# Half of the sums x1 + lam y of half 0 made beside y of half 1, from the x1 that is loaded there

## The chip, the cores and the metric

The kernel runs on one core of one Trainium2 chip. The metric is device time in microseconds, from one launch to its end; a kernel's time is the median of its runs. Beside the timed runs there is one profiled execution, taken by the hardware profiler, and all rows quoted here come from it. The engines are TensorE (PE, with its weight loads as PEld), VectorE (DVE), ScalarE (ACT), GpSimd (POOL) and SyncE (SP). SP and POOL issue most DMAs (rows named SPq are SP's issues).

## The reference, cut to what matters

The input is one image of 256 x 256 pixels and 128 channels in float32. Layer 0 is a row-wise attention with a residual; its result is `x1`. Layer 1 takes the group-normed `x1` as 256 tokens (its first axis), each an image of 256 x 128 points, runs a spectral attention over them and then two spectral mixing layers:

```python
attn = fno_layer(attn, p_wr, p_wi, p_bias, p_sw, p_sb, (H, W))
attn = instance_norm(attn + tokens, attn_norm_w, attn_norm_b)
attn = attn.reshape(b * (C // TOKEN_CODIM), TOKEN_CODIM, H, W)
h0 = instance_norm(attn, norm2_w, norm2_b)
h1 = fno_layer(h0, mix_wr[0], mix_wi[0], mix_bias[0], mix_sw[0], mix_sb[0], (H, W), norm=True, act=True)
h2 = fno_layer(h1, mix_wr[1], mix_wi[1], mix_bias[1], mix_sw[1], mix_sb[1], (H, W), norm=True)
out = instance_norm(h2, mon_w, mon_b) + attn
...
x = x + _L1_conv_ref(_gn(x), ...)
```

In the kernel's names `y` is `attn + tokens` before its instance norm (the group norm is folded into the matrices), and that norm is `lam y` plus a constant. The last two lines therefore need, at every pixel, the sum `w = x1 + lam y`; `lam` is one number per token, known only when all of a token's `y` has been made and its variance taken. `norm(h2)` is added to `w` at the very end.

## The kernel before

The 256 tokens are treated as two halves of 128 (`a` = 0 and 1), one token per partition. A half has 16 blocks of `NB` = 2048 pixels, or 32 half blocks `u` of `HB` = 1024. The order of each engine's instructions from `y_blocks` on is the order in which the Python code emits them (`manual_schedule`); the tile framework adds the semaphore waits, also those that come from memory which is used again: a pool that opens after another one has closed takes over its memory, and its first writes wait for the last use of what lay there.

The stages that matter here run in this order (L1813 on):

* `y_blocks(0, ...)`: y of half 0, 32 half blocks, kept whole in the SBUF tile `blocks` (16 x 2048 per partition; `hb[b]` is block b).
* `mp0`, the pool of the first modes: `y_blocks(1, br, 0, 24)` makes y of half 1 for u = 0 to 23, woven with `first_modes(0, ...)`. After that y goes on alone (`run(y1)`).
* `hp0`, the pool of the first images: `first_images(0, ...)`, 16 blocks.
* `mp1`: y of half 1 for u = 24 to 31 with `second_modes(0)` and `first_modes(1)`, then the images and outputs of both halves.

**y_blocks** (L1327). For a half block u, SP loads x1 of all 256 tokens (`load_x1`, tag "xt", three buffers, two loads of 512 KB each) and, every second u, the modes `gs`. The load for u + 2 is emitted at the top of u, so it reuses the buffer of u - 1. TensorE makes 16 products with `mpT` (L1351) and 16 small ones from the modes (L1219) into four PSUM banks; DVE scales them into y (L1361, `yt`) and takes statistics (L1363). For half 1, POOL then stores y to DRAM (L1365, `yd`, 512 KB).

**first_modes** (L1441) takes the variance of y of half 0, makes `lam` (column 3 of `h.col`) in a chain of small DVE steps with two square roots on ACT, scales F, and runs `mix_modes` (L1368): 16 products `x0m` (L1387), each summed into PSUM by TensorE (`x0acc`, L1400). Of the 16, those with number 2, 5, 8, 11 and 14 are on POOL, the others on DVE. `mixed` (L1405) copies the two sums into one tile `x0Z` of tag "f" (ACT L1410, DVE L1411), and `synth_modes` turns it into modes in four chunks (TensorE `g10gp` L609, copies `g10gt` of tag "gt" L617, stores to `Gd1` by POOL and ACT L622). `weave` (L1250) draws the next half block of y whenever the steps of the modes have used up the 4.2 us that a half block is counted with.

**first_images** (L1510) for half 0. Per block b: SP loads the modes `gs2` (L1243, four loads of 64 KB) and the two halves of x1 (`load_w`, L1530, 512 KB each, tiles of tags "yt" and "xw"); TensorE makes `ups` from block b (L1234 and L1219); ACT applies gelu in place into `blocks` (L1560); TensorE transposes the block before (`htps`, L1572), DVE copies it (L1584, L1575), TensorE makes `sps` (DVE statistics, L1592) and `psA` (L1595), ACT copies that into `yA` (L1597), POOL stores it (L1598, `Yd`). Beside this, `add_w` makes the sums w one block ahead, before gelu overwrites y: ACT scales y by lam (L1537), POOL adds the x1 (L1540) and stores the sum to the DRAM tile `wd` (L1541, 512 KB). Much later `output_0` loads `wd` again (L1733).

Of the kernel before, what the change touches and what calls it, by code (L numbers as in the profile page):

```python
# [18 lines left out]
P = 128  # L19
# [526 lines left out]
def layer1(tc, I, C, ident, x1d, upool, U, stats2, groups, out):  # L546
# [9 lines left out]
    with ExitStack() as ctx:  # L556
# [705 lines left out]
        def run(stage):  # L1262
            for _ in stage:
                pass
# [51 lines left out]
        for a in range(2):  # L1316
            h = Half()
            halves.append(h)
            h.col = sp.tile([P, 16], FP, name=f"col_{a}")
            h.turn = sp.tile([P, 8], FP, name=f"turn_{a}")  # L1320
            h.bl0 = sp.tile([P, P], FP, name=f"bl0_{a}")
            h.Gd1 = dram.tile([32, 4, 64, P], FP, name=f"Gd1_{a}")
            h.Gd2 = dram.tile([32, 4, 64, P], FP, name=f"Gd2_{a}")
            h.Yd = dram.tile([H, 32, P], FP, name=f"Yd_{a}")
        wd = dram.tile([P, 16 * NB], FP, name="wd")

        def y_blocks(a, psum, lo, hi, kept=16):  # L1327

            tt = slice(a * P, (a + 1) * P)
            gs = {}  # L1330

            def load(u):
                if (a, u) not in xts:
                    xts[a, u] = load_x1(a, u)
                if u % 2 == 0:
                    gs[u // 2] = xp.tile([P, 4, P], FP, tag="gs", name=f"gs_{a}_{u}", bufs=3)
                    load_modes(gs[u // 2], Gd0, u // 2, tt)

            load(lo)
            load(lo + 1)  # L1340
            yield 0.0
            for u in range(lo, hi):
                b, s = u // 2, u % 2
                if u + 2 < hi:
                    load(u + 2)
                xt = xts.pop((a, u))
                ps = [psum.pool.tile([P, 512], FP, tag=psum.tag, name=f"yps_{a}_{u}_{j}") for j in range(4)]
                ps = [z[:, 0:256] for z in ps]
                for j in range(4):
                    for sc in range(2):  # L1350
                        nc.tensor.matmul(  # L1351
                            rows_of(ps[j]), mpT[:, sc, tt], by_turn(xt[:, sc])[:, j],
                            start=(sc == 0), stop=False,
                        )
                image(ps, gs[b], bsy, range(2 * s, 2 * s + 2))
                if a == 0:
                    yt = blocks[:, b, s * HB : (s + 1) * HB]
                else:
                    yt = xp.tile([P, HB], FP, tag="yt", name=f"yt_{u}")
                for j in range(4):  # L1360
                    nc.vector.tensor_tensor(by_turn(yt)[:, j], rows_of(ps[j]), bc(rwb, 1, 2), ALU.mult)  # L1361
                for g in range(2):
                    nc.vector.bn_stats(ystat[:, a, 2 * u + g, :], yt[:, g * 512 : (g + 1) * 512])  # L1363
                if a:
                    nc.gpsimd.dma_start(ydv[:, a, u * HB : (u + 1) * HB], yt)  # L1365
                yield 4.2

        def mix_modes(mk, acc, F, l, tag, cs):  # L1368

# [71 lines left out]
        def first_modes(a, wp, mk, psum, gts):  # L1441

            h = halves[a]
            F = mk("F", [P, 4, 2, P], f"F0_{a}")
            nc.sync.dma_start(
                F.rearrange("p c r t -> p (c r) t"),
                Fyd[:, :, :, a * P : (a + 1) * P].rearrange("p c r t -> p (c r) t"),
            )
            dg = mk("m", [P, 2, P], f"dg3_{a}")
            ym, yv, ra, lam, r2, rho, sig = (h.col[:, k : k + 1] for k in range(7))  # L1450
            nc.vector.bn_aggr(h.col[:, 0:2], ystat[:, a].rearrange("p k s -> p (k s)"))
            yield 1.0
            rsqrt(nc, wp, ra, yv, EPS, "rq")
            nc.vector.tensor_mul(lam, ra, an[:, 0:1])
            nc.vector.tensor_mul(r2, lam, lam)
            nc.vector.tensor_mul(r2, r2, yv)
            yield 1.8
            rsqrt(nc, wp, r2, r2, EPS, "rq")
            nc.vector.tensor_mul(rho, lam, r2)
            nc.vector.tensor_mul(rho, rho, ch[:, 0:1])  # L1460
            nc.vector.tensor_mul(sig, ym, rho)
            nc.vector.tensor_sub(sig, ch[:, 1:2], sig)
            nc.vector.tensor_scalar(dg[:, 0, :], ident, rho, None, ALU.mult)
            nc.vector.tensor_scalar(dg[:, 1, :], ident, sig, None, ALU.mult)
            nc.vector.tensor_scalar(h.bl0, blk[0], rho, None, ALU.mult)
            yield 2.7
            ps = psum.tile(f"rhops_{a}")
            nc.tensor.matmul(ps[:, 0:256], ones, dg.rearrange("p k t -> p (k t)"), start=True, stop=True)
            yield 0.9
            rb = mk("m", [P, 256], f"rb_{a}")  # L1470
            nc.vector.tensor_copy(rb, ps[:, 0:256])
            f8 = F.rearrange("p c r t -> p (c r) t")
            nc.vector.tensor_tensor(f8, f8, bc(rb[:, 0:P], 1, 8), ALU.mult)
            nc.vector.tensor_add(F[0:1, 0, 0, :], F[0:1, 0, 0, :], rb[0:1, P:])
            yield 1.8
            acc = [psum.tile(f"x{a}acc_{r}") for r in range(2)]
            yield from mix_modes(mk, acc, F, 0, f"x{a}", range(4))
            Z, sq = mixed(mk, acc, f"x{a}")
            yield 1.2
            tail = norm(wp, mk, psum, h, sq, f"x{a}")  # L1480
            for c in range(4):
                synth_modes(wp, psum.pool, Z, P, h.Gd1, f"g1{a}", turned=True, chunk=c, ptag=psum.tag, gts=gts,
                            queues=(nc.gpsimd, nc.scalar))
                yield 2.4
                if c == 0:
                    yield next(tail)
                    yield next(tail)
                if c == 1:
                    run(tail)
                    nc.vector.tensor_mul(h.bl0, h.bl0, h.row[:, 0:P])  # L1490

                    ps = h.row
                    nc.tensor.matmul(ps[:, 256:257], blk[0], sig, start=True, stop=False)
                    nc.tensor.matmul(ps[:, 256:257], ident, ch[:, 2:3], start=False, stop=True)
                    nc.vector.tensor_copy(h.col[:, 13:14], ps[:, 256:257])
                    turned = mk("m", [P, 4, P], f"turned_{a}")
                    for j in range(4):
                        t = turned[:, j].rearrange("k (b d x) -> k b d x", b=2, d=2)
                        nc.vector.tensor_copy(
                            t[:, :: (-1 if j & 2 else 1), :: (-1 if j & 1 else 1)],  # L1500
                            ident.rearrange("k (b d x) -> k b d x", b=2, d=2),
                        )
                    for j in range(4):
                        nc.tensor.matmul(
                            ps[:, 260 + 2 * j : 262 + 2 * j], turned[:, j], h.col[:, 12:14],
                            start=True, stop=True,
                        )
                    nc.vector.tensor_copy(h.turn, ps[:, 260:268])

        def first_images(a, wp, yp, psk, pst, first=None):  # L1510
# [14 lines left out]

            def load_w(b):
                for s in range(2):
                    t = (yp, "yt", 2) if s == 0 else (wp, "xw", 1)
                    ys[b, s] = t[0].tile([P, HB], FP, tag=t[1], name=f"xw_{b}_{s}", bufs=t[2])
                    nc.sync.dma_start(ys[b, s], x1v[:, a, b * NB + s * HB : b * NB + (s + 1) * HB])  # L1530

            def add_w(b):

                t = yp.tile([P, NB], FP, tag="xt", name=f"w0_{b}", bufs=3)
                for s in range(2):
                    px = slice(s * HB, (s + 1) * HB)
                    nc.scalar.activation(t[:, px], hb[b][:, px], AF.Identity, scale=h.col[:, 3:4])  # L1537
                for s in range(2):
                    px = slice(s * HB, (s + 1) * HB)
                    nc.gpsimd.tensor_tensor(t[:, px], t[:, px], ys.pop((b, s)), ALU.add)  # L1540
                    nc.gpsimd.dma_start(wd[:, b * NB + s * HB : b * NB + (s + 1) * HB], t[:, px])  # L1541
# [271 lines left out]
        with tc.manual_schedule(engines=COMPUTE | {ENG.SP}):  # L1813
# [8 lines left out]
            with yctx:  # L1822
                U1 = 24
                with tc.tile_pool(name="mp0", bufs=1) as wp:
                    y1 = y_blocks(1, br, 0, U1)
                    weave((2.4 * t for t in first_modes(0, wp, tiles(wp), bq, [(wp, "gt", 1)])), y1)
                    run(y1)
                with tc.tile_pool(name="hp0", bufs=2) as wp:
                    run(first_images(0, wp, xp, bq, br))
# [226 lines left out]
```

## Time and profile before

| what | value |
|---|---|
| time, median of 3 runs | 2884.54 us (2880.02 to 2887.79) |
| the profiled execution's own time | 2878.79 us |
| its span | 2877.0 us |
| busy: PE, DVE, ACT, POOL | 2643.1, 2004.2, 1488.4, 1679.6 us |
| first and last y of half 1 in `mp0` (start of the DVE row) | 2036.4 and 2190.2 us |
| last row of half 0's images (psA) | 2327.0 to 2328.0 us |
| DMA of the span | 430.12 MB, 149 GB/s on average |

The span is the time between the first and the last instruction of the profiled execution; the device time lies 1.8 us above it. A row of the timeline has its start, its duration, the engine, the line, the operation with output and inputs, and in brackets how long the engine had been idle and what ended that. In a group's row, "busy" and "mean ns" are followed by the idle time before the group's instructions and its releasers. In the table by stretch there is one row per stretch of the span.

### The profile page before, as it was taken

Reading aid. Unit: us, or ns where it says so; the run is one execution under the profiler, and the core shown is the slowest. Engines: PE = TensorE matmul, PEld = TensorE weight load, DVE = VectorE, ACT = ScalarE, POOL = GpSimd, SP = SyncE. Lnnn points to the kernel's source line nnn. Section 1 sums busy time; section 2 is a strip of 40 time slices with the busy share of each in tenths; the row PEclk is TensorE's granted clock in tenths of the full one; section 3 lists DMA queues with packets and bytes.
Section 4 is the critical chain, followed back from the end, with each engine's and each line's share of the span. In section 5 each row is a group of like instructions: output and inputs, shape, how many; then the busy total and the mean of one; then the engine's idle time right before and its main releaser. Section 6 shows DMA issues by size and latency. Waiting matters only on the chain. (4 is left out here: it accounts for less than half of the span.)

```text
span 2877.0 us, 71481 instructions
## 1 busy us (share of the span) xinstructions
PE 2643.1 (92%) x29116; PEld 1935.1 (67%) x29116; DVE 2004.2 (70%) x3264; ACT 1488.4 (52%) x2847; POOL 1679.6 (58%) x1308
## 2 busy tenths in 40 slices
PE   7799999999999999999999989999889988799655
PEld 6677777777777777777777656778665555455533
DVE  7788888888888888888888854756645555365445
ACT  0477777777777777777777622200004611365132
POOL 0399999999999999999999900200114733111211
PEclk9999999999999999999999999999999999799865
DMA  9422222222222222222222101188879984798599
GB/s 369 166 67 67 67 67 67 67 67 67 68 67 67 67 67 67 67 67 67 67 67 67 47 22 54 34 276 274 281 243 312 311 304 134 253 363 306 187 360 339
DMA packets 246705, 430.12 MB, mean 149 GB/s; under 512 B 26278, under 2 KB 174201, under 8 KB 239976
## 3 DMA queue, kind: packets, MB, share of 16 engines
q1 hardware_dynamic: 206568, 335.34, 35.4%
q0 software_dynamic: 22912, 81.80, 7.4%
q10 hardware_dynamic: 16896, 8.39, 1.0%
q8 instruction: 231, 3.78, 0.6%
q14 instruction: 98, 0.80, 0.1%
HBM read 290.17 MB, written 135.27 MB: 148 GB/s over the span
## 5 line engine op out<-in xcount | busy, mean ns | idle before, releaser
L332 POOL TENSOR_TENSOR e<-e,b1T 128x1024 f32<-128x1024 f32 x256 | 606.1, 2367 | 164.6 <-PE u L381 90.3
L336 POOL TENSOR_TENSOR es<-e 128x512 f32<-128x512 f32 x512 | 639.6, 1270 | 20.1
L314 ACT ACTIVATE sc<-sc,b2T 128x512 f32<-128x512 f32 x512 | 339.0, 662 | 364.6 <-PE sc L305 356.2
L356 DVE RECIPROCAL av<-av 128x256 f32<-128x256 f32 x256 | 452.3, 1767 | 27.2 <-DVE og L355 1.4
L314 ACT ACTIVATE e<-sc,b2T 128x512 f32<-128x512 f32 x512 | 348.6, 681 | 0.0
L327 DVE TENSOR_TENSOR e<-sc,b1T 128x1024 f32<-128x1024 f32 x256 | 311.0, 1215 | 0.0
L305 PE MATMUL sc<-qkT 32*128 32x256 f32 x4096 | 293.4, 400 | 1.3 <-DVE e L327 1.3
L344 PE MATMUL av<-e,v 128*32 128x256 f32 x4096 | 274.7, 385 | 0.5 <-POOL e L332 0.5
L305 PEld LDWEIGHTS sc<-qkT 32*128 32x128 f32 x4096 | 185.1, 184 | 112.2 <-issue 97.7
L1351 PE MATMUL yps<-xt,mpT 128*128 128x256 f32 x1024 | 241.8, 389 | 19.4 <-DVE yt L1361 9.7
L355 DVE SCALAR_TENSOR_TENSOR og<-gate,av 128x256 f32<-128x256 f32 x256 | 107.7, 421 | 190.6 <-PE av L349 190.6
L1351 PEld LDWEIGHTS yps<-xt,mpT 128*128 128x128 f32 x1024 | 191.9, 192 | 56.7 <-DVE yt L1361 13.0
L1365 POOL DMA_DIRECT2D yd<-yt x32 | 17.7, 555 | 340.8 <-DVE yt L1361 340.8
L360 POOL TENSOR_TENSOR x<-xt,bo 128x256 f32<-128x256 f32 x256 | 187.7, 734 | 0.0
L279 PE MATMUL qk<-xnT,wT_wq 128*128 128x256 f32 x512 | 179.5, 432 | 1.7 <-ACT xnT L271 1.7
L285 PEld LDWEIGHTS gv<-wT_wv,kvT 128*128 128x128 f32 x1024 | 155.0, 192 | 13.3
L349 PE MATMUL av<-es,ones 128*32 128x256 f32 x2048 | 157.5, 379 | 2.5 <-POOL es L336 2.5
L366 PE MATMUL wo<-wT_wo,og 128*128 128x128 f32 x1024 | 156.8, 276 | 2.7 <-DVE og L357 2.7
L344 PEld LDWEIGHTS av<-e,v 128*32 128x32 f32 x4096 | 107.0, 109 | 76.1 <-POOL e L332 1.0
L381 PE MATMUL u<-adft,x 128*128 128x129 f32 x1024 | 156.4, 275 | 0.0
L285 PE MATMUL gv<-wT_wv,kvT 128*128 128x128 f32 x1024 | 156.0, 275 | 0.0
L1718 ACT ACTIVATE blocks<-h2ps,col 128x512 f32<-128x512 f32 x128 | 89.0, 779 | 129.4 <-PE h2ps L1219 129.4
(546 smaller groups left out, 5282.8 us busy)
## 6 DMA issues: line engine op xcount, KB each, us to landing
xt<-x1d SPq DMA_DIRECT2D x128, 512.0 KB, 5.9
xb<-in_x_dram SPq DMA_DIRECT2D x32, 1024.0 KB, 7.8
xt<-in_x_dram SPq DMA_DIRECT2D x128, 256.0 KB, 2.7
kt<-in_L_conv_kv_x_dram SPq DMA_DIRECT2D x128, 256.0 KB
x1d<-x SPq DMA_DIRECT2D x256, 128.0 KB, 2.3
y<-yd SPq DMA_DIRECT2D x62, 512.0 KB, 8.9
gs<-Gd SPq DMA_DIRECT2D x384, 64.0 KB, 5.1
yd<-yt POOLq DMA_DIRECT2D x32, 512.0 KB, 6.3
```

The lines of the kernel that those rows point to most:

```text
L279: nc.tensor.matmul(ps[:, 0:256], wT["wq"], xnT, start=True, stop=True)
L285: nc.tensor.matmul(ps[:, 256 + c * P : 256 + (c + 1) * P], kvT[:, c * P : (c + 1) * P], wT["wv"], start=True, stop=True,)
L305: nc.tensor.matmul(sc[h // 2][:, h % 2, c * 256 : (c + 1) * 256], qkT[p, 256 + c * P : 256 + (c + 1) * P], qkT[p, 0:256], start=True, stop ...
L314: nc.scalar.activation(r["e"][1][:, :, c, :] if hp else z, z, AF.Exp, bias=b2T[:, c, s : s + 1])
L327: nc.vector.tensor_tensor(r["e"][0].rearrange("p h c q -> p (h c q)"), r.pop("sc").rearrange("p h x -> p (h x)"), b1T[:, 0:2].rearrange("p ...
L332: nc.gpsimd.tensor_tensor(e1, e1, b1T[:, 2:4].rearrange("p h c q -> p (h c q)"), ALU.mult)
L336: nc.gpsimd.tensor_tensor(r["es"][hp], e[:, :, 0, :], e[:, :, 1, :], ALU.add)
L344: nc.tensor.matmul(ps[hd, 0:256], r["v"][:, c, hd], r["e"][h // 2][:, h % 2, c, :], start=(c == 0), stop=(c == 1),)
L349: nc.tensor.matmul(ps[32 * h : 32 * h + 32, 256:512], self.ones, r["es"][h // 2][:, h % 2, :], start=True, stop=True,)
L356: nc.vector.reciprocal(rd, rd)
L360: nc.gpsimd.tensor_tensor(r["x1"], r["x"], bc(self.bo, 1, 2), ALU.add)
L1351: nc.tensor.matmul(rows_of(ps[j]), mpT[:, sc, tt], by_turn(xt[:, sc])[:, j], start=(sc == 0), stop=False,)
```

## The change

`y_blocks` gets a callback that is called at the end of each half block, after y's store. For half 1 in `mp0` it is an object `Sums`. While `halves[0].sums` is set, it makes the sum of half 0 for the same u from the x1 that was just loaded for y (`xt[:, 0]` holds the tokens of half 0): ACT scales `blocks`, POOL adds `xt[:, 0]` and stores to `wd`, behind y's store in POOL's order. The three tiles that it uses in turn come from `mp0`'s tags "f" (one) and "gt" (two), in which the result of the modes and its copies lie at other times. The flag is set when `lam` is there, cleared when the products of the modes have been made, and set again when the modes are done; so the sums of u = 1 to 10 and 18 to 23 are made there, 16 in all. `load_w` and `add_w` of the images leave those out.

```diff
--- before.py
+++ after.py
@@ -1319,12 +1319,13 @@
             h.col = sp.tile([P, 16], FP, name=f"col_{a}")
             h.turn = sp.tile([P, 8], FP, name=f"turn_{a}")
             h.bl0 = sp.tile([P, P], FP, name=f"bl0_{a}")
+            h.sums, h.summed = False, set()
             h.Gd1 = dram.tile([32, 4, 64, P], FP, name=f"Gd1_{a}")
             h.Gd2 = dram.tile([32, 4, 64, P], FP, name=f"Gd2_{a}")
             h.Yd = dram.tile([H, 32, P], FP, name=f"Yd_{a}")
         wd = dram.tile([P, 16 * NB], FP, name="wd")
 
-        def y_blocks(a, psum, lo, hi, kept=16):
+        def y_blocks(a, psum, lo, hi, also=None):
 
             tt = slice(a * P, (a + 1) * P)
             gs = {}
@@ -1363,7 +1364,34 @@
                     nc.vector.bn_stats(ystat[:, a, 2 * u + g, :], yt[:, g * 512 : (g + 1) * 512])
                 if a:
                     nc.gpsimd.dma_start(ydv[:, a, u * HB : (u + 1) * HB], yt)
+                if also:
+                    also(u, xt)
                 yield 4.2
+
+        class Sums:
+
+
+
+            def __init__(self, wp):
+                self.wp, self.tiles = wp, []
+
+            def __call__(self, u, xt):
+                h = halves[0]
+                if not h.sums:
+                    self.tiles = []
+                    return
+                if not self.tiles:
+                    two = self.wp.tile([P, 2, HB], FP, tag="gt", name=f"w2_{u}", bufs=1)
+                    one = self.wp.tile([P, HB], FP, tag="f", name=f"w1_{u}", bufs=1)
+                    self.tiles = [two[:, 1], two[:, 0], one]
+                t = self.tiles.pop()
+                px = slice(u * HB, (u + 1) * HB)
+                nc.scalar.activation(
+                    t, blocks.rearrange("p b x -> p (b x)")[:, px], AF.Identity, scale=h.col[:, 3:4]
+                )
+                nc.gpsimd.tensor_tensor(t, t, xt[:, 0], ALU.add)
+                nc.gpsimd.dma_start(wd[:, px], t)
+                h.summed.add(u)
 
         def mix_modes(mk, acc, F, l, tag, cs):
 
@@ -1452,6 +1480,7 @@
             yield 1.0
             rsqrt(nc, wp, ra, yv, EPS, "rq")
             nc.vector.tensor_mul(lam, ra, an[:, 0:1])
+            h.sums = True
             nc.vector.tensor_mul(r2, lam, lam)
             nc.vector.tensor_mul(r2, r2, yv)
             yield 1.8
@@ -1475,6 +1504,7 @@
             yield 1.8
             acc = [psum.tile(f"x{a}acc_{r}") for r in range(2)]
             yield from mix_modes(mk, acc, F, 0, f"x{a}", range(4))
+            h.sums = False
             Z, sq = mixed(mk, acc, f"x{a}")
             yield 1.2
             tail = norm(wp, mk, psum, h, sq, f"x{a}")
@@ -1525,17 +1555,22 @@
 
             def load_w(b):
                 for s in range(2):
+                    if 2 * b + s in h.summed:
+                        continue
                     t = (yp, "yt", 2) if s == 0 else (wp, "xw", 1)
                     ys[b, s] = t[0].tile([P, HB], FP, tag=t[1], name=f"xw_{b}_{s}", bufs=t[2])
                     nc.sync.dma_start(ys[b, s], x1v[:, a, b * NB + s * HB : b * NB + (s + 1) * HB])
 
             def add_w(b):
 
+                todo = [s for s in range(2) if (b, s) in ys]
+                if not todo:
+                    return
                 t = yp.tile([P, NB], FP, tag="xt", name=f"w0_{b}", bufs=3)
-                for s in range(2):
+                for s in todo:
                     px = slice(s * HB, (s + 1) * HB)
                     nc.scalar.activation(t[:, px], hb[b][:, px], AF.Identity, scale=h.col[:, 3:4])
-                for s in range(2):
+                for s in todo:
                     px = slice(s * HB, (s + 1) * HB)
                     nc.gpsimd.tensor_tensor(t[:, px], t[:, px], ys.pop((b, s)), ALU.add)
                     nc.gpsimd.dma_start(wd[:, b * NB + s * HB : b * NB + (s + 1) * HB], t[:, px])
@@ -1822,8 +1857,9 @@
             with yctx:
                 U1 = 24
                 with tc.tile_pool(name="mp0", bufs=1) as wp:
-                    y1 = y_blocks(1, br, 0, U1)
+                    y1 = y_blocks(1, br, 0, U1, Sums(wp))
                     weave((2.4 * t for t in first_modes(0, wp, tiles(wp), bq, [(wp, "gt", 1)])), y1)
+                    halves[0].sums = True
                     run(y1)
                 with tc.tile_pool(name="hp0", bufs=2) as wp:
                     run(first_images(0, wp, xp, bq, br))
```

## The prediction

> **What bounds the kernel now.** I read the page first, then busy time by stretch of the span, the timeline of the stretches that the change touches, and the waits of TensorE in them. The chain that ended last begins near 2424 us, behind everything the change touches, so it says nothing here. From the page, the busy tenths (each digit 72 us):
>
> ```profile
> span 2877.0 us, 71481 instructions
> ...
> POOL 0399999999999999999999900200114733111211
> ...
> DMA  9422222222222222222222101188879984798599
> ```
>
> POOL is at 1 tenth in the two slices that hold most of half 1's y (29th and 30th digit, 2014 to 2158 us) and at 4 and 7 in the next two, where the images begin: that is the room the change uses. But DMA stands at 8 and 7 in the first two and at 9 in the others. By stretch (us; PE, PEld, DVE, ACT, POOL busy; granted clock, DMA share, GB/s):
>
> ```profile
> 2060.00:2108.00 48.00, 38.93 (x215) 24.54 (x213) 25.89 (x48) 1.18 (x2) 8.80 (x11) 1.00 0.64 215
> 2160.00:2180.00 20.00, 17.70 (x136) 14.16 (x140) 10.82 (x24) 0.15 (x1) 2.45 (x5) 1.00 1.04 348
> 2240.00:2260.00 20.00, 19.91 (x286) 10.62 (x288) 12.70 (x21) 14.37 (x19) 15.90 (x12) 1.00 0.91 308
> ```
>
> Three regimes. Plain y blocks (second row) take 4.87 us each, with TensorE and DMA both close to full. The y blocks woven with the mode products (first row) take 8.70 us: TensorE idles 9 of 48 us. In the images (third row) TensorE never rests. One woven block:
>
> ```profile
> 2078.72 0.73 PE L1219 MATMUL yps<-bsy,gs 32*128 32x128 f32 x16
> ...
> 2079.38 1.98 PE L1400 MATMUL x0acc<-x0m,ident 128*128 128x512 f32 x4
> 2079.46 1.42 DVE L1361 TENSOR_TENSOR yt<-yps,rwb 128x256 f32<-128x256 f32 x4 [3.40 <-PE yps L1219]
> ...
> 2081.18 0.59 POOL L1365 DMA_DIRECT2D yd<-yt  x1 [7.02 <-DVE yt L1361]
> 2081.80 1.06 POOL L1387 TENSOR_TENSOR x0m<-F,mixwr 128x512 f32<-128x512 f32 x1
> 2082.12 1.29 DVE L1387 TENSOR_TENSOR x0m<-F,mixwn 128x512 f32<-128x512 f32 x1
> 2082.91 0.30 PEld L1400 LDWEIGHTS x0acc<-x0m,ident 128*128 128x128 f32 x2 [2.38 <-POOL x0m L1387]
> 2082.91 1.12 PE L1400 MATMUL x0acc<-x0m,ident 128*128 128x512 f32 x2 [1.55 <-POOL x0m L1387]
> ```
>
> This is the crux: POOL's product x0m stands behind y's store in POOL's order, and TensorE already waits for it. TensorE's waits from 2034 to 2192 us (total, times, longest):
>
> ```profile
> PE x0acc L1400 <- POOL x0m L1387: 7.7, 5, 1.6
> ...
> PE g10gp L609 <- ACT x0sq L1416: 2.9, 1, 2.9
> ```
>
> What moves, as it costs in the images:
>
> ```profile
> L1540 POOL TENSOR_TENSOR w<-w,xw 128x1024 f32<-128x1024 f32 x32 | 75.6, 2364 | 16.3 <-DMA xw<-x1d 13.1 <-ACT blocks L1560 2.4 <-ACT w L1537 0.4
> ...
> L1541 POOL DMA_DIRECT2D wd<-w x32 | 18.1, 566 | 9.5 <-POOL w L1540 9.2 <-DMA xw<-x1d 0.3
> ```
>
> [...] the DVE product at 2082.12 takes 1.29 us beside POOL's product, 0.69 us alone. [...] it idles 2.94 us to 2109.54, and the granted clock of 2110 to 2114 is 0.62; behind 5.64 us of idle (to 2344.67) the 3.72 us of one block's products become about 7.
>
> **The change, part by part.** It moves 16 of 32 half-block sums (u = 1 to 10 and 18 to 23) from the images into y of half 1. Out: 16 loads of 512 KB on SP's queue. Moved: 16 ACT scalings (1.15 us), 16 POOL adds (2.36 us), 16 wd stores on POOL's queue (0.57 us and 0.30 us of wait). Added: the load of x1 for block u+3 waits for the add of u, and three waits on the sums' landing.
>
> Scalings: ACT is idle in y, the tiles come back two blocks ahead: 0 if the stores land in time, else in the range below.
>
> (a) *u = 1 to 5, plain blocks.* A block's add ends 1.72 (yt to store) + 0.55 + 2.36 = 4.7 us after yt starts. The load for u+3, issued before at the end of u's products, goes out about 6 us later and lands at +4.7 +0.8 (two issues) +6 (xt's median landing is 5.9) = 11.5, needed at 10.5: +1. The DVE chain of first_modes (two-input 128x1 steps at 2044.9 to 2047.5 and the 1.23 us F product) meets the adds of u = 1 and 3: up to 2.4 us late each. POOL's time itself, 3.8 of 4.87 us, is covered. I take +4 (0 to 8).
>
> (b) *u = 5 to 9, woven.* Behind each y store, ahead of x0m: 2.36 + 0.30 + 0.57 + 0.03 = 3.26 us, with no cover, since TensorE waits for exactly that product. 5 x 3.26 = +16.3. TensorE's idle grows from 1.55 to 4.8 us a block, beyond the gaps that dropped the clock above. A drop costs 1.5 us (2109) to 3.4 us (2344); I take 2 us five times: +10 (0 to 17).
>
> (c) *The modes' result.* x0Z lies in tag "f", where the sum of u = 10 was. ACT's and DVE's copies now wait for its wd store to land: yt(10) + 4.96 to issue + 5.5 (wd takes 4.0 to 8.1) = 10.5 instead of 2.66 us: +7.8 (6 to 9). Behind it stand the modes' squares, TensorE's g10gp, and in TensorE's order y of u = 11.
>
> (d) *u = 18 to 23, plain.* As (a) without the DVE chain: loads of 21 to 23 about 2 us late. Traffic per block grows from 1.70 to 2.23 MB; at the 348 GB/s of the row above that is 6.4 instead of 4.9 us, but the loads run two blocks ahead, so only part shows. +4 (0 to 10).
>
> (e) *The seam to the images.* The images' pool takes over the memory of the modes' pool. Its first load, gs2_0_0, was issued at 2176.75, well ahead; in the changed program it waits for the wd stores of u = 21, 22 and 23. The last lands near yt(23) + 4.96 + 4.5 = 9.5 (DMA is nearly idle then); four issues of 0.46 us and 2.5 us of landing (gs takes 1.8 to 9.4) make 13.5 us, against the first image product at yt(23) + 1.07. +12.4 (9 to 16), and +1 for a cold clock. On SP xw and the second gs stand behind it; they arrive in time for block 1.
>
> (f) *Images.* The period is 8.13 us on average (first transposes 2199.58 to 2321.58, 15 periods) and 7.41 us at best, where TensorE runs without a gap. Eight blocks' worth lose their sums: 8 x 0.72 = -5.8; I take -6 (-12 to 0). ACT (6.3 to 4 us a block) and POOL are not what ends a period.
>
> Sum: 4 + 16.3 + 10 + 7.8 + 4 + 13.4 - 6 = +49.5 us. The profiled execution took 2878.79 us (span 2877.0); its changed twin is near 2928. The median of the runs shown, 2884.54, lies 5.75 above it: **2934 us**.
>
> **Rivals.** *Mild*: the clock does not drop, loads and stores land early: 0 + 16.3 + 0 + 6 + 0 + 9 - 7 = +24, 2909 us. For it: five clean waits of 1.6 us without a drop; against: every gap over 2.9 us dropped it. *DMA becomes the bound of y*: with 1.04 of share already, the ten summed plain blocks pay the whole 6.4 - 4.9 = 1.5 us: +15 instead of (a) + (d) = 8, and landings of 8 us add 5 in (c) and (e): +62, 2946 us. *The other side, faster*: the images are held by the DMA's and POOL's backlog and not by TensorE's order, so that all 15 periods fall to 7.41 us (-10.8), and the sums fit into y. It decides at (b): only if POOL's 3.26 us hide inside the 1.55 us wait and (e) vanishes; nothing covers them, as the woven block shows. 2884.5 - 10.8 = 2874 us. That the change does not do what it says is excluded: the changed program holds 16 adds with xt and 16 loads fewer.
>
> **How the numbers follow.** My sum 0.5, mild 0.2, DMA bound 0.2, faster 0.05, and 0.05 for additions that cancel. A run of this kernel can tell about 0.3% (8.7 us) from no change. Range 2908 to 2957: from mild to the cold clock at 17 with late landings. Slower 0.90, same 0.05, faster 0.05.
>
> **What would show it.** Right: TensorE's wait for POOL's x0m rises from 7.7 to about 24 us; woven blocks of 12 us or more, some at a clock of 0.5 to 0.7; the wait ahead of g10gp near 10 us; a gap of 12 us ahead of the first image product, ended by gs; summed images at 7.4 to 7.8 us. Wrong: x0m's wait unchanged, or the images shorter by over 12 us.

## The result, and the profile after

The changed kernel takes 2921.73 us (median of six runs, 2914.53 to 2927.73), the kernel before 2881.15 us (six runs, 2875.28 to 2887.79). The ratio is 1.0138, with a 95% interval of 1.0126 to 1.0151: 40 us slower. The profiled execution of the changed kernel took 2927.68 us, the upper end of its runs, so the two traces differ by 49 us where the medians differ by 40.6.

From the page of the changed kernel (busy tenths, each digit 73 us):

```profile
span 2925.9 us, 71467 instructions
...
POOL 0399999999999999999999502100323433111211
...
DMA  9422222222222222222222101488666684898599
```

The stretch in question is the 29th to 34th digit. POOL went from 1, 1, 4, 7, 3, 3 to 3, 2, 3, 4, 3, 3: its work was moved as meant. DMA went from 8, 7, 9, 9, 8, 4 to 6, 6, 6, 6, 8, 4. In y_blocks line numbers are 1 higher than before, in the modes 28 and in the images 35.

One woven block of the changed kernel, from its timeline:

```profile
2095.35 1.98 PE L1428 MATMUL x0acc<-x0m,ident 128*128 128x512 f32 x4
2095.43 1.41 DVE L1362 TENSOR_TENSOR yt<-yps,rwb 128x256 f32<-128x256 f32 x4 [4.49 <-PE yps L1219]
...
2097.15 0.60 POOL L1366 DMA_DIRECT2D yd<-yt  x1 [9.07 <-DVE yt L1362]
2097.77 2.35 POOL L1392 TENSOR_TENSOR w<-w,xt 128x1024 f32<-128x1024 f32 x1
2098.09 2.59 DVE L1415 TENSOR_TENSOR x0m<-F,mixwn 128x512 f32<-128x512 f32 x1
...
2100.41 0.57 POOL L1393 DMA_DIRECT2D wd<-w  x1 [0.30 <-POOL w L1392]
...
2101.01 1.06 POOL L1415 TENSOR_TENSOR x0m<-F,mixwr 128x512 f32<-128x512 f32 x1
...
2102.12 1.70 PE L1428 MATMUL x0acc<-x0m,ident 128*128 128x512 f32 x2 [4.79 <-POOL x0m L1415]
...
2103.85 0.69 DVE L1415 TENSOR_TENSOR x0m<-F,mixwi 128x512 f32<-128x512 f32 x1 [3.18 <-PE x0acc L1428]
```

The reader sees 3.26 us between the end of y's store (2097.75) and the start of POOL's x0m (2101.01): the add, its wait and the store. TensorE is idle 4.79 us for it where it was 1.55. The products behind the gap take 1.70 us for what took 1.12: the granted clock is 0.57 from 2102 to 2106 us, where it was 1.00 over the five woven blocks before. DVE's product takes 2.59 us beside POOL's add, and 0.69 where POOL has nothing to do (last row). The five woven blocks take 13.6 to 14.2 us each.

TensorE's waits from 2034 to 2240 us in the changed kernel (total, times, longest):

```profile
PE x0acc L1428 <- POOL x0m L1415: 23.9, 5, 4.8
PE g10gp L609 <- DVE x0Z L1441: 12.0, 1, 12.0
...
PE yps L1352 <- DMA xt<-x1d: 4.5, 4, 1.6
```

The wait for x0m rose from 7.7 to 23.9 us, the one ahead of g10gp (the first products that need x0Z) from 2.9 to 12.0, and a wait for the loads of x1 is new. The timeline shows where the wait ahead of g10gp comes from, and the seam to the images:

```profile
2141.29 0.57 POOL L1393 DMA_DIRECT2D wd<-w  x1 [0.30 <-POOL w L1392]
2147.89 0.58 ACT L1438 COPY x0Z<-x0acc 128x512 f32<-128x512 f32 x1 [39.12 <-DMA wd<-w]
2148.01 0.69 DVE L1439 COPY x0Z<-x0acc 128x512 f32<-128x512 f32 x1 [8.96 <-DMA wd<-w]
...
2241.76 0.57 POOL L1393 DMA_DIRECT2D wd<-w  x1 [0.30 <-POOL w L1392]
2244.82 1.73 SPq L1243 DMA_DIRECT2D gs<-Gd  x4
...
2246.75 3.49 PE L1219 MATMUL ups<-k_bsyn,gs 32*128 32x128 f32 x32 [8.76 <-DMA gs<-Gd]
```

Both copies of x0Z wait for the landing of a wd store, 6.6 us after its issue. At the seam the last wd store goes out at 2241.76; the modes of the first image are issued 3.06 us later, and TensorE has been idle for 8.76 us when they arrive. Its first products then take 3.49 us at a clock of 0.50; the same 32 products took 1.17 us at 1.00 in the kernel before (at 2191.31).

The images, by stretch, from the first transposes of block 0 to those of block 15 (us; PE, PEld, DVE, ACT, POOL busy; granted clock, DMA share, GB/s), first before, then after. A period is the time from one block's first transposes to the next block's:

```profile
2199.58:2321.58 122.00, 119.50 (x1740) 63.02 (x1736) 73.21 (x120) 79.04 (x102) 97.01 (x74) 0.99 0.94 318
```

```profile
2257.10:2366.10 109.00, 109.00 (x1740) 54.52 (x1736) 72.83 (x120) 65.52 (x89) 53.38 (x43) 1.00 0.65 209
```

All 15 periods, also those of blocks whose two sums were not moved, became 7.41 us (7.47 the first; the last is 5.22, as it was before), and TensorE has no gap left.

By stage (us, from the starts of y's DVE rows and of the blocks' first transposes; the parts are those of the prediction):

| stage | part | before | after | change | predicted |
|---|---|---|---|---|---|
| y of u = 0 to 5 | (a) | 25.70 | 31.14 | +5.4 | +4 |
| u = 5 to 10, woven | (b) | 43.42 | 69.10 | +25.7 | +26.3 |
| u = 10 to 11, x0Z | (c) | 11.97 | 21.50 | +9.5 | +7.8 |
| u = 11 to 18 | | 48.02 | 48.35 | +0.3 | 0 |
| u = 18 to 23 | (d) | 24.69 | 30.69 | +6.0 | +4 |
| u = 23 to first transposes | (e) | 9.34 | 20.25 | +10.9 | +13.4 |
| 15 image periods | (f) | 122.00 | 109.02 | -13.0 | -6 |
| sum | | | | +44.8 | +49.5 |

The remaining 4 us up to 48.9 lie behind the images. From the last y of half 1 (u = 31) to the end, the profiled executions of before, the change and the nine experiments that leave that stretch as it was take 496.2 to 501.2 us without order, so this is the spread of single executions.

### The profile page after: what moved, and what is told of

It is laid out like the page before. It is cut to its first block, busy times and chain, and to the rows that moved or that the text cites. A ratio compares the mean times of both kernels' runs of the same rounds, so it can differ in the third digit from the quotient of the medians.

```text
span 2925.9 us, 71467 instructions
## 1 busy us (share of the span) xinstructions
PE 2651.2 (91%) x29116; PEld 1935.9 (66%) x29116; DVE 2016.6 (69%) x3264; ACT 1487.5 (51%) x2847; POOL 1679.9 (57%) x1308
## 5 line engine op out<-in xcount | busy, mean ns | idle before, releaser
L1352 PE MATMUL yps<-xt,mpT 128*128 128x256 f32 x1024 | 252.5, 401 | 27.3 <-DVE yt L1362 11.6
L1352 PEld LDWEIGHTS yps<-xt,mpT 128*128 128x128 f32 x1024 | 199.4, 200 | 70.7 <-DVE yt L1362 14.8
L285 PEld LDWEIGHTS gv<-wT_wv,kvT 128*128 128x128 f32 x1024 | 155.0, 192 | 13.4
```

Of the source, the lines that this page charges most:

```text
L285: nc.tensor.matmul(ps[:, 256 + c * P : 256 + (c + 1) * P], kvT[:, c * P : (c + 1) * P], wT["wv"], start=True, stop=True,)
L1352: nc.tensor.matmul(rows_of(ps[j]), mpT[:, sc, tt], by_turn(xt[:, sc])[:, j], start=(sc == 0), stop=False,)
```

## The experiments

"On before" below means the ratio to the kernel before times 2881 us, with its 95% interval. Times of a stage come from one profiled execution each.

### Half of the change at a time: first_ten and last_six

```diff
-                    halves[0].sums = True      (first_ten: ahead of run(y1))
-            h.sums = True                      (last_six: behind lam in first_modes)
```

> Only the sums of u = 1 to 10 move; those of 18 to 23 stay in the images. If the parts of the change add up by stage, the delays read from the changed kernel's trace stay as they are up to u = 11: +5 us (plain blocks 1 to 5), +26 (woven blocks) and +9.5 (x0Z), +40 at the start of u = 11; the blocks from 18 on and the seam cost nothing (first image product 1 us behind u = 23 as before); the images win back 4 us if only the summed blocks get shorter (5 blocks of 0.7 us), up to 9 if a backlog is what lengthens them. Together +31 to +36 us on before. Rival: the late stages catch up with what the first ten lose, because they were limited by loads: +25 or less.

> Only the sums of u = 18 to 23 move. Theory of separate parts: woven blocks at 8.7 us and x0Z 2.7 us behind u = 10 as before; +6 us from u = 18 to 23, +11 at the seam (TensorE's wait for the first gs of the images 9 us or more), minus 2 us (three summed blocks of 0.7) up to minus 8 in the images: +9 to +15 us on before. Rival, that the seam's gap comes from the lateness of everything ahead of it: no wait of more than 3 us at the seam, total within 4 us of before.

Measured: first_ten 2912.84 us, ratio 1.0101 (1.0083 to 1.0119), +29 us; last_six 2889.76 us, 1.0018 (1.0009 to 1.0027), +5 us. Stage by stage first_ten keeps (a) +4.7, (b) +24.1, (c) +9.3, has (d) at +0.5 and (e) at -0.15, and its images take 111.64 us (-10.4, more than the 9 expected). The whole is 2 us under the low end of what was expected. last_six has (a) and (b) at 0, (c) at +1.2 and +1.5 from u = 11 to 18 (not an effect of the sums: traffic_only below, which leaves y as it was, has the same +1.2 and +1.5), (d) +3.9, (e) +11.8 with the same wait of 8.9 us for gs, and images of 114.03 us (-8.0). The two add up to +34 on before where the change has +40: by stage the costs add, but the gains in the images do not (-10.4 and -8.0 against -13.0 together). Ten sums win 1.04 us each, six 1.33, sixteen 0.81. The rivals (late stages that catch up, a seam that is only the lateness of what is ahead) fall by the stages. last_six came out 4 us under the low end of what was expected, and 5 us under its own sum of stages.

### POOL's order in the woven blocks: sum_after_x0m

The add and the store are held back until POOL's next x0m has been emitted (or until the next load would overwrite their x1):

```diff
-                nc.gpsimd.tensor_tensor(t, t, xt[:, 0], ALU.add)
-                nc.gpsimd.dma_start(wd[:, px], t)
+                self.held.append(add)        # the two lines above
+                if not self.mixing:
+                    self.flush()
...
                         made[:, q * n : (q + 1) * n], bc(f, 3, 4), bc(w, 2, G), ALU.mult
                     )
+                    if adder and (k + q) % 3 == 2:
+                        adder.flush()
```

> POOL's add and store of a sum are emitted behind the next POOL product x0m instead of ahead of it (u = 5 to 9); all else as in the change. Theory of POOL's order: TensorE's wait for x0m falls from 24 us to 8 or less, the gaps become too short for the clock to drop, and the woven blocks take 8.7 to 10.5 us instead of 13.8: 16 to 25 us less than the changed kernel, +16 to +24 on before. Rival[...]: the add now stops DVE's products x0m as long, TensorE waits for those instead (a new wait x0acc <- DVE x0m of 2 us a block), woven blocks stay above 11.5 us and at most 12 us are won.

Measured: 2895.35 us, 1.0042 (1.0026 to 1.0059), +12 us on before and 28 less than the change, more than the 16 to 25 expected. The five woven blocks take 43.19 us (before 43.42, the change 69.10): all of (b) is gone, and the clock over them is 1.00 (the change 0.83). TensorE's waits and one block:

```profile
PE x0acc L1444 <- POOL x0m L1429: 7.4, 5, 1.5
```

```profile
2086.66 1.06 POOL L1429 TENSOR_TENSOR x0m<-F,mixwr 128x512 f32<-128x512 f32 x1
2087.05 3.55 DVE L1429 TENSOR_TENSOR x0m<-F,mixwn 128x512 f32<-128x512 f32 x1
2087.67 2.36 POOL L1399 TENSOR_TENSOR w<-w,xt 128x1024 f32<-128x1024 f32 x1
2087.78 0.30 PEld L1444 LDWEIGHTS x0acc<-x0m,ident 128*128 128x128 f32 x2 [2.31 <-POOL x0m L1429]
2087.78 1.12 PE L1444 MATMUL x0acc<-x0m,ident 128*128 128x512 f32 x2 [1.49 <-POOL x0m L1429]
```

The same add now runs 2087.67 to 2090.03, and half of the rival came true: DVE's product, which runs beside x0m and then beside the add, takes 3.55 us (0.69 in the change where POOL has nothing to do). But it ends at 2090.60, and the products that TensorE sums next start at 2092.94 (TensorE makes the next y first), so nobody waits. The position in POOL's order was the cause, not POOL's amount of work, which is the same.

### The clock's share: kept_busy

```diff
+                    if none is not None and (k + q) % 3 == 2:
+                        for n4 in range(24):
+                            z = acc[0 if k + q == 2 else 1][:, n4 % 4 * P : (n4 % 4 + 1) * P]
+                            nc.tensor.matmul(z, ident, none, start=False, stop=False)
```

> The change, with 24 products of the unit matrix with a 128x128 tile of zeros put into TensorE's order ahead of each x0acc that waits for POOL (5 places; they add nothing to the sums, about 0.13 us each, 3.1 us a place). They fill most of the 4.8 us in which TensorE otherwise idles. If 9.5 of the 25.7 us of the woven blocks are the clock, the granted clock there stays near 1.0 and a woven block takes 11.9 to 12.4 us instead of 13.8: 7 to 10 us less than the changed kernel, +31 to +34 on before. Rival: the blocks take longer than POOL's 3.26 us [...]; then they stay above 13.3 us, and the time within 3 us of the change's.

Measured: 2912.34 us, 1.0102 (1.0080 to 1.0124), +29 us on before, 10 less than the change. The woven blocks take 12.24 us, 60.90 for the five. Forty us of them, first in the change, then here:

```profile
2080.00:2120.00 40.00, 25.64 (x110) 15.77 (x109) 17.69 (x24) 3.33 (x3) 13.73 (x12) 0.83 0.50 164
```

```profile
2080.00:2120.00 40.00, 40.00 (x289) 33.26 (x289) 20.19 (x25) 3.34 (x3) 16.73 (x15) 1.00 0.53 179
```

More work on TensorE made the block 1.6 us shorter, with the clock at 1.00 instead of 0.83. The filling took 5.5 us a place, not the 3.1 that was reckoned, and ends some 0.4 us behind POOL's x0m; so the clock's part of (b) is estimated at the 8.2 us won or a little more. Of the 3.54 us a block that remain above 8.70, POOL's add, its wait and its store are 3.26. The rival (DVE's products, longer beside POOL's, as the reason) asked for blocks above 13.3 us and falls.

### The two waits for late stores: nine_and_three

```diff
+        KEEP = {*range(1, 10), *range(18, 21)}
-                if not h.sums:
+                if not h.sums or u not in KEEP:
```

> The change without the sums of u = 10 and of u = 21 to 23 (they stay in the images; twelve are moved). Tile f is then free early, and the last store of a moved sum is issued three blocks ahead of the images. If x0Z waits for the store of u = 10, u = 11 starts 12 us behind u = 10 again and not 21 (-9); if the images' first modes wait for the last three stores, the gap of 9 us at the seam goes, the clock with it (-11), and u = 18 to 23 cost 1 us instead of 6 (-5). The images keep at least 11 of their 13 us, since ten sums moved alone won 10.4. Together 23 to 25 us less than the changed kernel: +15 to +18 on before. Rival: stores of the earlier sums are late too; then a wait of 3 us or more for a wd store stays in either place, and less than 18 us are won.

Measured: 2900.83 us, 1.0065 (1.0046 to 1.0084), +19 us on before, 21 less than the change where 23 to 25 were expected. (c): u = 10 to 11 takes 11.67 us again, and the wait ahead of g10gp is the old one:

```profile
PE g10gp L609 <- ACT x0sq L1446: 2.9, 1, 2.9
```

(e): from u = 23 to the first transposes 9.80 us (before 9.34), with no wait for gs. Both causes are thus shown by taking away what was waited for. The images keep their 109.03 us with twelve sums moved. What failed is (d): u = 18 to 23 take 30.23 us, as much with three sums as with six.

### Three sums: three

```diff
+        KEEP = {18, 19, 20}        (used as in nine_and_three)
```

> Only the sums of u = 18, 19 and 20 move. No cost at the seam, 0 to +1 us from u = 18 to 23. If the images are held by a backlog of traffic, even three sums win more than their own 3 x 0.36 us: -3 to -6 us in the images, so -2 to -6 in all. If every sum wins only its own share: -1 us, not to be told from before.

Measured: 2880.87 us, 0.9990 (0.9979 to 1.0000): not to be told from before. The images win 8.3 us (113.69) with three sums moved of 32, more than expected, and (d) takes 5.6 of them back (30.29), also against what was expected; 1.1 and 1.5 us more were lost from u = 10 to 18, as in last_six and in traffic_only. Where the 5.6 come from shows best in behind_and_three below, which has the same three sums. First its timeline, then two rows by stretch:

```profile
2169.07 5.73 SPq L1017 DMA_DIRECT2D xt<-x1d  x4
...
2174.64 0.70 PE L1354 MATMUL yps<-xt,mpT 128*128 128x256 f32 x2 [0.50 <-DVE yt L1364]
...
2176.94 4.98 PE L1354 MATMUL yps<-xt,mpT 128*128 128x256 f32 x14 [1.60 <-DMA xt<-x1d]
```

```profile
2174.64:2176.94 2.30, 0.70 (x2) 0.30 (x3) 2.22 (x5) 0.00 (x0) 1.18 (x3) 1.00 1.05 362
2176.94:2179.40 2.46, 2.46 (x6) 2.01 (x7) 0.00 (x0) 0.59 (x1) 2.16 (x2) 0.54 1.01 390
```

The load for u = 21 goes out when the add of u = 18 has ended (2169.05), 5.3 us after TensorE was done with that x1, and with the DMA at a share of 1.0 it lands 7.9 us later, 1.6 us too late. TensorE then runs at a clock of 0.54. The same happens at u = 23 (1.75 us idle, then 14 products in 4.85 us, the clock 0.50 at first). Here a late load costs 1.6 to 1.8 us of idling and 1.7 of clock (14 products in 4.98 us; at the clock of 1.00 that would be 14/16 of 3.72, 3.26 us). In the run three and in the change, three loads are late from u = 18 on (TensorE waits 0.45, 0.96 and 2.02 us in the one, 0.55, 1.25 and 1.58 us in the other), and each time only one of the three gaps is followed by slow products (4.98 us for 14, behind 2.02 us of idling in the one and 1.25 in the other). So three sums bring as many late loads as six.

### What holds the images: images_sixteen, modes_ahead, traffic_only, adds_only

Before, TensorE's weight loads waited for the modes 16 times in the images. These waits lie in nine of the blocks, not in 16 of 16 as the expectation of modes_ahead has it. Waits of all engines in the images of the kernel before:

```profile
ACT yA L1597 <- DMA Yd<-yA: 23.9, 11, 3.4
...
POOL w L1540 <- DMA xw<-x1d: 11.6, 16, 2.3
PEld ups L1234 <- ACT w L1537: 10.9, 13, 0.8
PEld ups L1219 <- DMA gs<-Gd: 10.9, 16, 1.4
```

Four edits of the kernel before:

```diff
 images_sixteen, in load_w (add_w then skips these too):
+                    if 2 * b + s in LEFT:
+                        continue
 modes_ahead:
-                    load(b + 1)
+                    load(b + 2)        (gs2 from tag "gs", three buffers)
 traffic_only:
-                    nc.gpsimd.tensor_tensor(t[:, px], t[:, px], ys.pop((b, s)), ALU.add)
 adds_only:
-                        load_w(b + 1)
-                    nc.gpsimd.dma_start(wd[:, b * NB + s * HB : b * NB + (s + 1) * HB], t[:, px])
```

> The kernel before, with the 16 sums of u = 1 to 10 and 18 to 23 left out of the images and made nowhere; the last stage loads x1 in their place, the same bytes in two DMAs. This measures what the images win alone, without a delay or a gap ahead of them. If a block wins only by its own sums: 15 periods from 122.0 to 116 us (-6). If the images are held by the traffic as a whole: all periods near 7.41 us, 109 to 111 us (-11 to -13). Rival: in the changed kernel the images are fast because the gap ahead of them let the queues run empty; then the first blocks stay above 8 us here and the sum is -6 or less. The end of the kernel moves by the same amount, within 3 us.

> The kernel before, no sum moved, but in the images of half 0 the modes gs2 are loaded two blocks ahead instead of one, in the three buffers that y used for its modes. It asks what held the images at 8.13 us a block. If it is that the modes land late behind the traffic of x1 and wd (PEld ups waits for gs in 16 of 16 blocks, 10.9 us in all), the period falls towards 7.41 us; 39.2 MB of these blocks at the 348 GB/s of the busiest row are 112.6 us, so -5 to -9 us in the images and in all. If the buffers of x1 and w, or POOL, are what is late, nothing changes (within 2 us), and a wait for ACT's w or for xw takes the place of the one for gs.

> The kernel before, with POOL's add left out of all 32 sums in the images; the loads of x1, ACT's scalings and the stores to wd stay, so wd holds lam y alone. The traffic is that of before, POOL has 75 us less to do. If the traffic holds the images at 8.13 us a block, they stay within 3 us of before (first products of psA 123 us from first to last). If POOL's adds and what queues behind them on POOL (the stores of wd and Yd) hold them, the periods fall to 7.4 to 7.6 us and 8 to 13 us are won.

> The kernel before, with the loads of x1 and the stores to wd left out of all 32 sums in the images; ACT's scalings and POOL's adds stay (an add takes the same tile twice), and the last stage reads x1 in place of wd. POOL has its adds, the DMA 1 MB instead of 2.5 MB a block. If the traffic holds the images, every period is 7.41 us (-13). If POOL does, they stay above 8 us on average and less than 3 us are won.

Measured: images_sixteen (its sums are made nowhere) 2863.30 us, 0.9945 (0.9926 to 0.9964); its 15 periods take 109.03 us, the first 7.47. So the gap at the seam is not what made the images fast in the change; taking out the sums is, and it wins all 13 us.

modes_ahead: 2883.04 us, 0.9997 (0.9988 to 1.0005), no change. TensorE no longer waits for gs (of the 10.9 us of its weight loads 6.7 remain, 8 gaps of 0.84 us, which blocks of 7.41 us have as well), and the first five periods are 7.4 us, but another wait takes its place (waits in its images):

```profile
ACT yA L1601 <- DMA Yd<-yA: 37.4, 12, 4.4
...
POOL w L1542 <- DMA xw<-x1d: 12.5, 12, 2.4
PEld htps L1576 <- ACT yA L1601: 12.2, 7, 2.8
```

The stores Yd stand behind the sums in POOL's order and land late; ACT can't write yA, and TensorE's weight loads wait for ACT, 12.2 us where they had no such wait before. The late modes were a symptom. traffic_only takes 2863.25 us, 0.9925 (0.9906 to 0.9944), its periods 109.30 us; adds_only 2867.00 us, 0.9937 (0.9920 to 0.9955), 109.04 us. (The whole times of these three fell by 16 to 22 us, more than the images' 13. In the profiled executions of traffic_only and adds_only the stretch from the images to the last y of half 1 is 4 us shorter too, and adds_only loses 6 us behind it, where its last stage reads x1; this was not followed.) By stretch, traffic_only and then adds_only:

```profile
2200.00:2310.00 110.00, 110.00 (x1776) 55.56 (x1760) 70.96 (x117) 80.73 (x104) 26.66 (x44) 0.99 1.02 374
```

```profile
2200.00:2310.00 110.00, 110.00 (x1747) 55.52 (x1746) 73.73 (x121) 79.56 (x103) 64.28 (x44) 1.00 0.30 88
```

All of the traffic fits into 7.41 us a block without the adds (374 GB/s, a share of 1.02), and the adds fit without the traffic. The second is a weaker test: the add of one tile to itself takes 1.88 us instead of 2.36, and POOL has no stores wd to issue, so it is busy for 64.28 us where it was busy for 97.01 before. What remains is that the two wait for each other, and the waits of the kernel before show it in both directions. Beside POOL's 11.6 us of waiting for xw stands this one of SP's queue, from 2199 to 2321 us:

```profile
SPq L1530 <- POOL w L1540: 38.9, 15, 3.3
```

A load of x1 lands, POOL's add waits for it with the stores of wd and Yd behind it, and the next load waits for the buffer that the add frees, 15 times. That this loop, and not POOL's whole load of adds and stores, sets the period is read from these waits; a second buffer for xw, which would test it, was not run. The loop would also explain why three sums win 8 us: in that run the first four periods are 7.4 to 7.5 us, four of 7.7 to 9.4 follow, and from there on, where blocks 9 and 10 lack their sums, all are 7.41 but the last, also those behind them. The loop falls behind within a few blocks, and a block or two of slack reset it for some time. That last step is read from the order of the periods, not shown by a run of its own.

### Sums where there is room: behind_and_three and behind_five

Both are sum_after_x0m with a KEEP: {5 to 9, 18 to 20} and {5 to 9}.

> Eight sums only, where the runs so far found room: u = 5 to 9 with POOL's part behind the next x0m, and u = 18 to 20. No sum beside the DVE chain of the modes (u = 1 to 4), none of u = 10 in tile f, none in the last three blocks. Stage by stage: 0 to +1 us up to u = 5, 0 in the woven blocks, 0 at x0Z (its tile held the sum of u = 8), 0 to +1 from u = 18, 0 at the seam, and -8 to -11 in the images (six sums moved won 8.0, ten won 10.4). Together -6 to -11 us, 2870 to 2875 us where before has 2881: faster than both kernels. Rival: eight sums spread over blocks 2, 3, 4, 9 and 10 leave the first and last images as slow as before; then -5 or less. Second rival: a new wait (the copies g10gt, whose tile gt held the sum of u = 9, or late loads of x1) gives it back: 0 or slower.

> Only the sums of u = 5 to 9, with POOL's part behind the next x0m; none in plain blocks. The three sums of u = 18 to 20 cost 5 to 7 us there, since the loads of x1 for u = 21 and 23 came 1.6 us late and each such gap brought half-clock products (4.98 instead of 3.72 us): without them u = 18 to 23 take 24.5 us again. Woven blocks 8.6 us, x0Z and the seam as before. The images win 8 to 11 us (three sums won 8.3, ten 10.4). Together -8 to -12 us on before, 2 to 4 us less than the eight sums by stages. Rival: moved sums of u = 18 to 20 are what emptied the queues at the start of the images, and five sums of blocks 2 to 4 win only their own share: -2 to -4 us.

Measured: behind_and_three 2871.20 us, 0.9961 (0.9948 to 0.9973), -11 us on before; behind_five 2873.10 us, 0.9964 (0.9952 to 0.9977), -10 us. Both beat both kernels; whole times can't tell them from each other. By stage the eight sums have (a), (b), (c) and (e) within 0.3 us of before, +7.4 in (d), and -13.0 in the images; the five have every stage of y within 0.4 us of before and -8.7 in the images (113.30). From u = 0 to the last y of half 1 that is 337.5 and 333.7 us (before 343.8). The wait for POOL in behind_five:

```profile
PE x0acc L1446 <- POOL x0m L1431: 7.4, 5, 1.5
```

The rival for behind_five (five sums win only their own share) falls, and the second one for behind_and_three holds in part: late loads of x1 took 7.4 us, though not all of the gain. (From u = 0 to the last y that is -6 us for the eight sums and -10 for the five; the -11 of the eight by the medians is 5 us more than its profiled execution shows.)

## Why the prediction was right, and where it was off

**Direction and range.** 2921.73 us lies in the range of 2908 to 2957 and 12 us below the 2934 forecast. Of the 12, 3.4 us are the median of before, which came down from 2884.54 to 2881.15 with more runs and took with it the correction of 5.75 us; 4.7 are the sum by stage (44.8 instead of 49.5). The rest is the place of the profiled executions in their spreads, and what lies behind the images. That the sum by stage came so near is in part luck: (a), (c) and (d) were 5 us larger than taken, (e) and (f) 9.5 us smaller.

**The signs named in advance.** Of those for being right, the wait for x0m (23.9 us), the woven blocks (13.6 us or more, clock 0.57) and the wait ahead of g10gp (12.0) came true; the gap ahead of the first image product was there, ended by gs, at 8.76 us instead of 12. One of the two signs of being wrong came true as well: the images are shorter by over 12 us.

**(b)** was right in mechanism and size: 16.2 us more of waiting for x0m against 16.3, and 9.5 us left for the clock against 10. sum_after_x0m shows that the order is the whole cause, kept_busy that 8 us or a little more of it came through the clock.

**(c)** was right in mechanism (nine_and_three); the landing took 6.6 us instead of the 5.5 taken, 1.1 of the 1.7 us by which +9.5 exceeds +7.8. **(e)** was right in mechanism (nine_and_three, last_six) and too large: wd landed 3.06 us after its issue instead of 4.5, and the four loads of gs took 1.9 us from the first issue to the first product instead of 4.3, so that the gap was 8.76 us instead of 12.4. The lower clock (0.50) cost 2.3 us there (3.49 instead of 1.17) instead of 1; the sum was 10.9 instead of 13.4.

**(a)** came to +5.4, with 3.2 to 5.1 in four other runs with these sums. It is nil in behind_and_three, which has none of u = 1 to 4. How it divides can be read from the changed kernel's rows. A 128x1 step of the DVE chain (L40) takes 1.43 us instead of 0.16 beside the add of u = 1, and the product of F (L1502) 2.62 instead of 1.23 beside that of u = 3; the next y starts 1.3 and 1.1 us later for it. The x1 of u = 5 lands late: 1.18 us of waiting and 14 products in 4.96 us instead of 3.26, 3.1 us in all, with a clock of 0.66 over those products. So the chain cost 2.3 us (the 2.4 us each was the author's estimate, the length of an add), and the late load was foreseen (+1), but not the clock behind it. **(d)** was mis-sized in its form: +6.0 against 4, but not in proportion to the sums. It is late loads, some with a lower clock behind them (0.65 after the idling of 1.25 us), not traffic per block.

**(f)** is the term that was wrong: -13.0 against -6, beyond the end of its own range. The step that failed is "Eight blocks' worth lose their sums: 8 x 0.72", and with it that "ACT (6.3 to 4 us a block) and POOL are not what ends a period". The slowness of a block was not the cost of its own sums: images_sixteen frees all 15 periods with half of the sums gone, and three and behind_five most of them with three and five. It fits a loop of loads, adds and stores that falls behind, so that breaking it in a few blocks frees others; that account is read from the waits. A smaller part is the average: 8.13 us takes in the last period of 5.22, which can't get shorter. The other fourteen average 8.34 us, 0.93 above 7.41, and eight blocks' worth of that would have been 7.5. So the rival "faster" was right on the images (its -10.8, from the same average, was -13.0) and fell where the prediction had put its decision: at (b) and (e), where nothing covers POOL's 3.26 us. "Mild" fell with the clock (0.83 over the woven blocks). "DMA bound" took 15 us for (a) and (d), which came to 11.4, and landings of 8 us, which were 6.6 in (c) and 3.1 in (e).

## What to carry to other kernels

Work moved onto an idle engine can cost more than its whole duration if it stands ahead of the one product that another engine waits for, and nothing if it stands behind it (25.7 us and 0 here): look at the queue at that place, not at the busy share. Memory taken over from a closed pool, or a buffer used again, made a late store somebody's first wait here (12.0 us ahead of g10gp, 8.76 at the seam), so stop such stores a few blocks ahead of a seam. And a stage with a small slowness in every block may be a loop that falls behind: freeing a few blocks can win most of it (five sums of 32 won 8.7 us of the 13), so try a few before you move half.

## What the runs showed of the hardware

The granted clock was lower after shorter idling of TensorE than the 2.94 and 5.64 us in the prediction, and not every time. In behind_and_three 0.50 us idle, 0.70 us of products and 1.60 us idle were followed by a clock of 0.54. In the changed kernel the same pattern ended once with 1.25 us idle and once with 1.58:

```profile
2222.54:2224.48 1.94, 0.70 (x2) 0.29 (x2) 1.91 (x5) 0.00 (x0) 0.69 (x2) 1.00 1.05 399
2224.48:2229.39 4.91, 4.91 (x15) 3.76 (x15) 0.31 (x1) 0.00 (x0) 2.77 (x2) 0.65 1.04 392
2230.61:2232.89 2.28, 0.70 (x3) 0.30 (x3) 2.22 (x5) 2.08 (x2) 1.02 (x2) 1.00 0.38 155
2232.89:2236.11 3.22, 3.22 (x15) 2.58 (x15) 0.00 (x0) 0.00 (x0) 2.44 (x2) 1.00 0.40 165
```

The shorter gap was followed by a clock of 0.65, the longer one by 1.00. In the woven blocks of before, gaps of 1.5 us with 7 us of products between them kept it at 1.00. So the length of the last gap alone doesn't decide; what else does was not measured.

DVE's product x0m takes 0.69 us in the changed kernel where POOL has nothing to do. It took 2.59 us beside POOL's add, and 3.55 us in sum_after_x0m, where it ran beside x0m and the add in turn. It ended about 0.56 us after the add each time, and the add took 2.35 to 2.36 us in both. In sum_after_x0m DVE's product starts at 2087.05, while POOL's x0m runs (from 2086.66, 1.06 us) and ahead of POOL's add (from 2087.67, 2.36 us), and yet it ends 0.57 us behind the add. The woven block before shows the same (3.53 us, 0.55 us behind the add), and behind_and_three has four such products of 3.53 us. What makes DVE's product last that long was not measured.
